# Differential attention: sums of softmax weights added on DVE before one product with ones, in a kernel of four layers

## The chip, the cores and the metric

The kernel runs on one core of a Trainium2 chip. The metric is the device time of one launch in microseconds, the median of several runs. Engines are named as in the profile: PE is TensorE (its weight loads are PEld), DVE is VectorE, ACT is ScalarE, POOL is GpSimd, SP is SyncE, which issues transfers.

## The reference

Four layers, each with a layer norm in front and a residual behind: a linear recurrence with gates (attn_a), a feed-forward layer with weights of three values (ffn), a differential softmax attention (attn_b), and the feed-forward layer again. Activations are 2 batches of 1024 rows by 512 features. The change touches attn_b alone:

```python
q = jnp.concatenate([q1, q2], axis=1)            # 32 query heads of 32
k2 = jnp.repeat(k, 2, axis=1)                    # 16 key heads, each used twice
v2 = jnp.repeat(v, 2, axis=1)
scores = jnp.einsum('bhqd,bhkd->bhqk', q, k2) * scale
scores = jnp.where(causal, scores, finfo.min)
p = jax.nn.softmax(scores, axis=-1)
y = jnp.einsum('bhqk,bhkd->bhqd', p, v2)
y1, y2 = (y[:, :H], y[:, H:])
lam = jax.nn.sigmoid(x @ Wlam)...
y = y1 - lam * y2
return y @ Wo
```

## The kernel before

The attention stage lies between about 734 and 1686 us of the span. It works through 32 *pairs* (`pairs`, L819), one for each batch b, group g of heads (four; two with q1, two with q2), p (which two of the group's key heads) and par (which of the group's two tiles of queries), four to a group. A sequence of 1024 is taken in key blocks kb of 128 and in two halves qb of queries. A pair has six *steps* of two key blocks each: two steps for the first half (qb = 0, kb 0 and 2) and four for the second (qb = 1, kb 0, 2, 4 and 6); the last two of a half lie at the diagonal.

In a step PE does, in this order, which is written out by hand for PE (`manual_schedule` of PE, L1298):

- the row phase (`row_phase`, L1002): scores into PSUM (L1024), then the row maxima subtracted by a product with ones (L1034). ACT takes the exponential into a tile of weights `pr` (L1056, four buffers); on blocks at the diagonal POOL cuts what is not causal (L1064); then POOL adds the weights of the second key block to those of the first (L1088);
- the banks of scores for the row maxima of the *following* pair (`maxima_bank`, L933, matmul L947), which DVE reduces (L958 with the causal mask on the diagonal, L963 without). `split_maxima` (L972; DVE L978 and L980, POOL L983 to L987) and `turn_maxima` (L990; PE transposes L994, DVE copies `mt` to SBUF in L996) hand them on;
- the weighing of the step before (`weigh`, L1091): products of the weights (first the second block's, then the added ones, except where kb is 0) with the values (tile `val`) into the first half of a PSUM bank, and a product of the added weights with ones (tile `summed`) into the second half, which gives the softmax's denominators. Both are L1109. After the last step of a query half ACT copies the bank (`ys`, L1128), and SP sends the denominators to `tot` (L1137) and the result to `share` (L1144);
- what is put beside a step by `at` (L1220 on): in two pairs of every group but the last, three projections each of queries or keys for the next group (`project`, L874, matmul pq L880) after steps 0, 2 and 4; transposes of the maxima; work of the second batch's input.

PSUM holds seven of these banks, handed out in rotation, so that a bank's next use waits for whoever reads it last. The orders of DVE, ACT, POOL and SP are decided by the framework's scheduler; only in the tail is DVE's written by hand too. At the end of a batch `divide` (L1149) turns the denominators into factors (DVE reciprocal L1156, multiply L1158, copy L1162, subtract L1163), `combine` (L1165) spreads them by a product `r` (L1170) over the shares (DVE L1173, POOL subtracts in L1174), and `project_part` (L1183, L1187) makes the output projection. `first_input` (L1199) prepares the input of the last layer in a room borrowed from the query buffers.

Outside this stage L224 and L514 to L519 belong to the first layers (quantizing weights, the recurrence).

Of the kernel before, what the change touches and what calls it, by code (L numbers as in the profile page):

```python
# [17 lines left out]
P = 128  # L18
D = 512
# [23 lines left out]
def kernel(  # L43
# [725 lines left out]
    with ExitStack() as s:  # L769
# [37 lines left out]
        for i in range(4):  # L807
# [10 lines left out]

        pairs = [  # L819
            (b, g, p, par)  # L820
            for b in range(NT // SEQ) for g in range(NG) for p in range(2) for par in range(2)
        ]
        groups, nmax, lams, totals, shares, factors = {}, {}, {}, {}, {}, {}

# [49 lines left out]
        def project(b, g, kind, e, w):  # L874


            n = f"{b}_{g}_{kind}"
            po = ring_bank(f"pq{n}_{e}")
            for k in range(NKC):
                nc.tensor.matmul(  # L880
                    po, w[:, k, ts(kind, P)], xts[b][:, k, ts(e, BLK)],
                    start=(k == 0), stop=(k == NKC - 1),
                )
            if e == 0:

                pool = (b_d, b_a, b_p)[kind]
                groups[b, g, kind] = pool.tile(
                    [P, 2, SEQ], F32, tag=f"group{kind}", name=f"gr{n}", bufs=2
                )
            made = groups[b, g, kind][:, :, ts(e, BLK)]  # L890
            if kind == 2:
                nc.scalar.copy(made[:, 0, :], po)
            else:
                nc.scalar.mul(made[:, 0, :], po, 1.0 / math.sqrt(HD))
            for i in range(2):
                nc.sync.dma_start(out=made[ts(i, 64), 1, :], in_=made[ts(1 - i, 64), 0, :])
# [7 lines left out]
        def name(pair):  # L904
# [19 lines left out]
        max_banks = [  # L924
# [6 lines left out]
        ]  # L931
# [70 lines left out]
        def row_phase(pair, following, step):  # L1002
# [47 lines left out]
            def weights(i, e):  # L1050
                if i not in room:
                    room[i] = b_a.tile(
                        [P, 2, BLK], F32, tag="pr", name=f"pr{name(pair)}_{made[i][0]}", bufs=4
                    )
                width = made[0][3] + made[1][3] if joined else made[i][3]
                nc.scalar.activation(room[i][:, e, :width], banks[i, e][:, :width], AF.Exp)  # L1056
# [27 lines left out]
                cut(1)  # L1084
            first, second = part(0), part(1)
            both = first[:, :, made[1][2] - made[0][2] :]
            for e in ((slice(0, 2),) if joined else range(2)):
                nc.gpsimd.tensor_add(both[:, e], both[:, e], second[:, e])  # L1088
            return [(pair, step, first, second)]

        def weigh(pair, step, first, second):  # L1091

# [5 lines left out]
                outs[pair] = edge_bank(f"y{name(pair)}_{qb}")  # L1098
            y, total = outs[pair][:, : BLK // 2], outs[pair][:, BLK // 2 :]
            last = kb == (qb + 1) * QB - 2  # L1100
            products = [(val[:, kb], first, lo0, y), (None, first, lo0, total)]
            products.insert(2 if kb == 0 else 0, (val[:, kb + 1], second, lo1, y))

            for n_product, (values_of, moving, lo, into) in enumerate(products):
                for half in range(2):
                    for e in range(2):
                        rows = ts(2 * half + e, HD)
                        head = summed if values_of is None else values_of[:, ts(4 * g + 2 * p + e, HD)]
                        nc.tensor.matmul(  # L1109
                            into[rows, lo // 2 :].rearrange("p (a r) -> p a r", r=64),  # L1110
                            head,
                            moving[:, e, :].rearrange("p (a h r) -> p a h r", h=2, r=64)[:, :, half, :],
                            start=(kb == 0 and n_product == 0),
                            stop=last and n_product > 0,
                            skip_group_check=True,
                        )
            if not last:
                return
            ys = b_c.tile([P, BLK], F32, tag="ys", name=f"ys{name(pair)}_{qb}", bufs=2)
            c = g % 2  # L1120
            if par == 0 and p == 0 and g % 2 == 0 and qb == 0:
                if g == 0:
# [20 lines left out]
            for half in range(2):  # L1143
# [2 lines left out]
                    in_=ys[ts(half, 64), : BLK // 2].rearrange("p (a r) -> p a r", r=64),  # L1146
                )

        def divide(b, e):  # L1149

            part = totals[b][:, ts(e, BLK)]

            pieces = 1 if b else NKC
            for i in range(pieces):
                piece = part[:, ts(i, BLK // pieces)]
                nc.vector.reciprocal(piece, piece)  # L1156
            second = part[rows_of[1]]
            nc.vector.tensor_mul(second, second, lams[b][rows_of[1], ts(e, BLK)])  # L1158
            factors[b, e] = b_c.tile([96 + NH, BLK], F32R, tag="factors", name=f"factors{b}_{e}")
            nc.gpsimd.memset(factors[b, e].bitcast(F32), 0.0)  # L1160
            hi, lo = (factors[b, e][64 * i : 64 * i + 32 + NH] for i in range(2))
            nc.vector.tensor_copy(hi, part)  # L1162
            nc.vector.tensor_sub(lo, part, hi.bitcast(F32))  # L1163

        def combine(b, c, e):  # L1165

            y1, y2 = (shares[b, half][:, c, ts(e, BLK)] for half in range(2))
            for half, y in enumerate((y1, y2)):
                r = ring_bank(f"r{b}_{c}_{e}_{half}")
                nc.tensor.matmul(  # L1170
                    r, head_of[:, half, c, :], factors[b, e], start=True, stop=True
                )
                nc.vector.tensor_mul(y, y, r)  # L1173
            nc.gpsimd.tensor_sub(y1, y1, y2)  # L1174

        def load_out(b):
            w_o = b_c.tile([P, NKC, D], F32, tag="w_vo", name=f"w_o{b}")
# [5 lines left out]
        def project_part(b, j, k, w_o, psum=ring_bank):  # L1183
            if k == 0:
                outputs[j] = psum(f"b_out{b}_{j}")
            po = outputs[j]
            nc.tensor.matmul(  # L1187
                po, shares[b, 0][:, k, ts(j, P)], w_o[:, k, :],
                start=(k == 0), stop=(k == NKC - 1),
            )  # L1190
            if k == NKC - 1:
                xi = xres[b * NQ + j]
                nc.vector.tensor_add(xi, xi, po)
# [26 lines left out]
        for n, pair in enumerate(pairs):  # L1220
# [4 lines left out]
                at(n + 1, 0, split_maxima, following, 1)  # L1225

            nb, ng = divmod(4 * b + g + 1, NG)
            if p == 0 and nb < NT // SEQ:
                def part(kind, e, nb=nb, ng=ng):
                    return lambda: project(nb, ng, kind, e, held["w", nb, ng])  # L1230
                if par == 0:
                    at(max(n - 1, 0), 0, lambda nb=nb, ng=ng: hold(("w", nb, ng), load_weights, nb, ng))

                for i in range(3):
                    at(n, 2 * i, part((2, 0, 1)[(3 * par + i) // 2], (par + i) % 2))
            if following:
                at(n, 4, turn_maxima, following, 0)
            if n:
                at(n, 0, turn_maxima, pair, 1)

            if g == 2 and p == 1 and b + 1 < NT // SEQ:
                if par == 0:
                    at(n, 0, normal_stats, b + 1)
                for t in range(4):
                    at(n, 2 * (t // 2), normalise, b + 1, 4 * par + t, ring_bank)
            if g == 3 and p == 1 and b + 1 < NT // SEQ:
                if par == 0:
                    at(n, 0, lambda b=b: hold(("v", b + 1), load_values, b + 1))
                else:

                    for j in range(NQ):
                        at(n + 1, 0, lambda b=b, j=j: values(b + 1, j, held["v", b + 1]))
                    at(n + 1, 0, lambda b=b: hold(("o", b), load_out, b))
                    at(n + 1, 1, divide, b, 0)
                    at(n + 1, 1, lambda b=b: lambdas(b + 1))
                    for c in range(NKC):
                        at(n + 1, 2 + c // 2, combine, b, c, 0)

                    at(n + 1, 3, divide, b, 1)
                    for c in range(NKC):  # L1260
                        at(n + 1, 4 + c // 2, combine, b, c, 1)

                    for j in range(NQ):
                        m, t = (n + 1, 5) if j < 2 else (n + 2, (j - 2) // 3)
# [132 lines left out]
```

## Time and profile before

| | us |
|---|---|
| median of 3 runs | 2048.32 |
| lowest and highest | 2045.67, 2051.11 |
| profiled execution | 2050.75 |
| its span | 2049.0 |
| PE busy in it | 2022.5 |
| POOL busy | 784.6 |
| DVE busy | 1101.0 |
| mean granted clock | 0.996 |

The span runs from the first to the last instruction of the profiled execution; 1.75 us of its time lie around it. A line of a group gives line, engine, operation, output and inputs with their sizes, how many, then busy time and mean duration, then the idle time of the engine ahead of them with who ended it. A line of the timeline gives start, duration, engine, line, operation, sizes and in brackets the idle time before it and who ended it; xN are N instructions that follow one another. Windows give for each stretch the length, the busy time of PE, PEld, DVE, ACT and POOL with numbers of instructions, then the granted clock, the share of the DMA engines and GB/s.

### The profile page before, as it was taken

The page shows a single profiled execution, that of the slowest core. Times are in us where ns is not written, and L with a number is a line of the kernel's source. Part 1 is how long each engine was busy: PE and PEld are TensorE (multiplying, and loading weights), DVE is VectorE, ACT ScalarE, POOL GpSimd, SP SyncE. Part 2 cuts the span into 40 slices and gives each one's busy share as a digit, 9 for nine tenths or more (in the row PEclk, how much of TensorE's full clock was granted, in tenths as well). Part 3 has the DMA queues.
Part 4 walks back from the last instruction along what each step waited for, and adds up shares of the span by engine and source line. Part 5 has one row for each costly group of instructions (what it writes and reads, how often), then busy time and mean ns, then how long its engine had stood idle before and what let it go on. Part 6 is the DMA issues. An engine that isn't in the chain of part 4 may idle for free.

```text
span 2049.0 us, 34958 instructions
## 1 busy us (share of the span) xinstructions
PE 2022.5 (99%) x13824; PEld 1290.9 (63%) x13832; DVE 1101.0 (54%) x2375; ACT 818.2 (40%) x1453; POOL 784.6 (38%) x1131
## 2 busy tenths in 40 slices
PE   8999999999999999999999999999999999999998
PEld 4444444788888854555555545565556648888887
DVE  5876868444344434555565556455556554343422
ACT  4444343234333422444444423254444513343433
POOL 1412323122222222666666635365657732222222
PEclk9999999999999999999999999999999999999999
DMA  7121212500000111111111101202110032000000
GB/s 278 65 92 62 88 57 80 222 0 1 1 1 1 37 48 34 48 28 43 28 43 28 43 9 39 60 22 51 25 30 15 15 149 103 21 1 21 0 21 21
DMA packets 77651, 99.14 MB, mean 48 GB/s; under 512 B 41520, under 2 KB 49840, under 8 KB 77488
## 3 DMA queue, kind: packets, MB, share of 16 engines
q1 hardware_dynamic: 77488, 96.92, 14.4%
q8 instruction: 108, 1.77, 0.4%
q14 instruction: 55, 0.45, 0.1%
HBM read 58.75 MB, written 16.78 MB: 37 GB/s over the span
## 4 chain that ended last, share of the span: by engine, by line
PE 92%; DVE 5%; POOL 1%; issue 1%; ACT 1%; DMA 0%; SPq 0%; DVEq 0%; ACTq 0%; POOLq 0%
PE g L664 11%; PE u L664 11%; PE f_out L685 11%; PE y L1109 11%; PE s L947 9%; PE pq L880 8%; PE t L1024 8%; PE pv L842 3%; PE pq L328 3%; PE a_out L546 2%; PE b_out L1187 2%; PE pv L328 2%; PE pa L328 2%; PE pg L328 2%; PE pk L328 2%; PE t L1034 1%
## 5 line engine op out<-in xcount | busy, mean ns | idle before, releaser
L1056 ACT ACTIVATE pr<-t 128x512 f32<-128x512 f32 (+1 forms) x640 | 306.6, 558 | 347.5 <-PE t L1034 294.2
L679 POOL TENSOR_TENSOR ssq<-ssq,sq 128x512 f32<-128x512 f32 x120 | 154.5, 1288 | 589.6 <-ACT sq L678 589.6
L1088 POOL TENSOR_TENSOR pr<-pr,pr 128x384 f32<-128x384 f32 (+1 forms) x256 | 287.1, 1132 | 121.5 <-ACT pr L1056 114.3
L963 DVE TENSOR_REDUCE nmax<-s 128x1 f32<-128x384 f32 (+1 forms) x320 | 183.2, 581 | 201.5 <-PE s L947 200.9
L958 DVE CUSTOM_DVE_ANT_0 s<-s,causal 128x512 f32<-128x512 f32 (+3 forms) x512 | 245.6, 506 | 54.0 <-PE s L947 49.6
L947 PE MATMUL s<-gr,gr 32*128 32x384 f32 (+3 forms) x1664 | 264.0, 480 | 1.9 <-DVE nmax L963 1.9
L670 DVE TENSOR_TENSOR h<-h,u 128x512 f32<-128x512 f32 x128 | 88.1, 688 | 317.5 <-PE u L664 305.4
L664 PE MATMUL g<-xs,w 128*128 128x512 f32 x1024 | 257.7, 394 | 0.0
L685 PE MATMUL f_out<-w,hs 128*128 128x512 f32 x1024 | 254.3, 390 | 0.3 <-DVE hs L673 0.3
L664 PE MATMUL u<-xs,w 128*128 128x512 f32 x1024 | 253.2, 389 | 0.0
L1024 PE MATMUL t<-gr,gr 32*128 32x512 f32 (+3 forms) x1536 | 224.3, 528 | 1.3 <-DVE nmax L963 1.3
L664 PEld LDWEIGHTS u<-xs,w 128*128 128x128 f32 x1024 | 192.2, 188 | 40.6
L685 PEld LDWEIGHTS f_out<-w,hs 128*128 128x128 f32 x1024 | 191.5, 188 | 40.7 <-DVE hs L673 1.1
L664 PEld LDWEIGHTS g<-xs,w 128*128 128x128 f32 x1024 | 190.0, 188 | 39.6 <-issue 1.0
L947 PEld LDWEIGHTS s<-gr,gr 32*128 32x128 f32 x1664 | 172.5, 186 | 45.5 <-issue 15.3
L1109 PE MATMUL y<-pr,val 128*32 128x256 f32 (+3 forms) x3072 | 188.1, 334 | 2.5 <-POOL pr L1088 1.9
L880 PE MATMUL pq<-b_xt,w_qk 128*128 128x512 f32 x384 | 176.0, 603 | 0.8 <-DVE nmax L958 0.8
L1064 POOL TENSOR_SCALAR_AFFINE_SELECT pr<-pr 128x256 f32<-128x256 f32 x256 | 101.9, 410 | 194.5 <-ACT pr L1056 190.9
L672 ACT CAST hs<-h 128x512 fp32r<-128x512 f32 x128 | 79.4, 620 | 234.7 <-DVE h L670 234.7
L669 ACT ACTIVATE h<-g 128x512 f32<-128x512 f32 x128 | 76.6, 599 | 230.5 <-PE g L664 230.4
L1109 PEld LDWEIGHTS y<-pr,val 128*32 128x32 f32 x3072 | 80.3, 109 | 89.4 <-issue 49.7
L673 DVE TENSOR_TENSOR hs<-h,hs 128x512 fp32r<-128x512 f32 x128 | 88.6, 692 | 87.2 <-ACT hs L672 87.2
(169 smaller groups left out, 2555.0 us busy)
## 6 DMA issues: line engine op xcount, KB each, us to landing
w<-w_kept SPq DMA_DIRECT2D x32, 768.0 KB
w_kept<-w SPq DMA_DIRECT2D x16, 768.0 KB
gr<-gr SPq DMA_DIRECT2D x96, 128.0 KB
w<-in_w_gu_dram SPq DMA_DIRECT2D x32, 256.0 KB
share<-ys SPq DMA_DIRECT2D x128, 64.0 KB
x<-in_x_dram SPq DMA_DIRECT2D x16, 256.0 KB
w<-in_w_pt_dram SPq DMA_DIRECT2D x16, 256.0 KB
w_qk<-in_wq_dram SPq DMA_DIRECT2D x8, 512.0 KB
```

The costliest lines, as they stand in the source:

```text
L328: nc.tensor.matmul(po, w[:, k, ts(c, P)], xt[:, k, :], start=(k == 0), stop=(k == NKC - 1))
L664: nc.tensor.matmul(po, ws[f][:, part, ts(k, P)], xs[:, e, k, :], start=(k == 0 and e == 0), stop=(k == NKC - 1 and e == 1),)
L679: nc.gpsimd.tensor_add(ssq, ssq, sq)
L685: nc.tensor.matmul(po[j], hp[:, e, ts(j, P)], ws[f][:, 2, :], start=(f == 0 and e == 0), stop=(f == NF - 1 and e == 1),)
L880: nc.tensor.matmul(po, w[:, k, ts(kind, P)], xts[b][:, k, ts(e, BLK)], start=(k == 0), stop=(k == NKC - 1),)
L947: nc.tensor.matmul(part, queries[:, ts(j, P)], keys[:, first * P : (first + nk) * P], start=True, stop=True,)
L958: nc.vector.tensor_tensor_reduce(part, part, causal[:, BLK - part.shape[-1] :], -1.0, 3.0e38, ALU.add, ALU.min, top,)
L963: nc.vector.tensor_reduce(top, part, AX.X, ALU.max, negate=True)
L1024: nc.tensor.matmul(banks[i, e][:, at_col : at_col + nq], keys[:, ts(kb, P)], queries[:, (qb + 1) * BLK - nq : (qb + 1) * BLK], start=True, ...
L1056: nc.scalar.activation(room[i][:, e, :width], banks[i, e][:, :width], AF.Exp)
L1088: nc.gpsimd.tensor_add(both[:, e], both[:, e], second[:, e])
L1109: nc.tensor.matmul(into[rows, lo // 2 :].rearrange("p (a r) -> p a r", r=64), head, moving[:, e, :].rearrange("p (a h r) -> p a h r", h=2, ...
```

## The change

For the second half of the queries the weights of steps 2 and 3 (kb = 0 and 2, full width) no longer have a product with ones each. `weigh` keeps the added weights of step 2 (`whole`), adds them to those of step 3 by a DVE add of 128x1024, and gives the sum one product with ones at the next step. The tiles `pr` therefore get six buffers. In the last pair DVE and not POOL adds the weights of the second block to the first (`adder`). The order of the pairs has par outside p; the projections stand in the second and third pair of a group; the query groups share three buffers and the key groups two. Two of the maxima steps have their banks in another order. The reciprocals are made in quarters (`invert`), placed step by step, and `combine` writes its difference into the other buffer (y2), which `project_out` reads.

```diff
-            for b in range(NT // SEQ) for g in range(NG) for p in range(2) for par in range(2)
+            for b in range(NT // SEQ) for g in range(NG) for par in range(2) for p in range(2)
...
-                pool = (b_d, b_a, b_p)[kind]
-                groups[b, g, kind] = pool.tile(
-                    [P, 2, SEQ], F32, tag=f"group{kind}", name=f"gr{n}", bufs=2
+                tag, bufs = ("keys", 2) if kind == 2 else ("queries", 3)
+                groups[b, g, kind] = b_p.tile(
+                    [P, 2, SEQ], F32, tag=tag, name=f"gr{n}", bufs=bufs
...
-            [(0, 0, "j4a"), (1, 0, "j01"), (0, 1, "j6a")],
-            [(1, 0, "j4a"), (0, 0, "j46"), (1, 1, "j5a")],
+            [(0, 0, "j4a"), (0, 1, "j6a"), (1, 0, "j01")],
+            [(1, 0, "j4a"), (1, 1, "j5a"), (0, 0, "j46")],
...
-                        [P, 2, BLK], F32, tag="pr", name=f"pr{name(pair)}_{made[i][0]}", bufs=4
+                        [P, 2, BLK], F32, tag="pr", name=f"pr{name(pair)}_{made[i][0]}", bufs=6
...
+            adder = nc.gpsimd if following else nc.vector
             for e in ((slice(0, 2),) if joined else range(2)):
-                nc.gpsimd.tensor_add(both[:, e], both[:, e], second[:, e])
+                adder.tensor_add(both[:, e], both[:, e], second[:, e])
...
+        whole = {}
...
-            products = [(val[:, kb], first, lo0, y), (None, first, lo0, total)]
-            products.insert(2 if kb == 0 else 0, (val[:, kb + 1], second, lo1, y))
+            sums = [(None, first, lo0, total)]
+            if qb and kb < QB:
+                sums = []
+            elif qb and kb == QB:
+                sums.insert(0, (None, whole.pop(pair), 0, total))
+            products = [(val[:, kb], first, lo0, y), *sums]
+            products.insert(len(products) if kb == 0 else 0, (val[:, kb + 1], second, lo1, y))
...
+            if qb and kb < QB:
+                if kb:
+                    nc.vector.tensor_add(first, first, whole[pair])
+                whole[pair] = first
...
+        def invert(b, e, i, pieces=NKC):
+            piece = totals[b][:, ts(e * pieces + i, BLK // pieces)]
+            nc.vector.reciprocal(piece, piece)
+
         def divide(b, e):
...
-            pieces = 1 if b else NKC
-            for i in range(pieces):
-                piece = part[:, ts(i, BLK // pieces)]
-                nc.vector.reciprocal(piece, piece)
...
-            nc.gpsimd.tensor_sub(y1, y1, y2)
+            nc.gpsimd.tensor_sub(y2, y1, y2)
...
-            room = b_d.tile([P, NKC, D], F32, tag="group0", name="xn_f1_0", bufs=2)
+            room = b_p.tile([P, NKC, D], F32, tag="queries", name="xn_f1_0", bufs=3)
...
-            if p == 0 and nb < NT // SEQ:
+            m = 2 * par + p
+            if m in (1, 2) and nb < NT // SEQ:
...
-                if par == 0:
-                    at(max(n - 1, 0), 0, lambda nb=nb, ng=ng: hold(("w", nb, ng), load_weights, nb, ng))
+                if m == 1:
+                    at(n - 1, 0, lambda nb=nb, ng=ng: hold(("w", nb, ng), load_weights, nb, ng))
                 for i in range(3):
-                    at(n, 2 * i, part((2, 0, 1)[(3 * par + i) // 2], (par + i) % 2))
+                    at(n, 2 * i, part((2, 0, 1)[(3 * (m - 1) + i) // 2], (m - 1 + i) % 2))
...
-                    at(n + 1, 1, divide, b, 0)
+                    for i in range(NKC):
+                        at(n, 3 + i // 2, invert, b, 0, i)
+                        at(n + 1, 1 + i // 2, invert, b, 1, i)
+                    at(n + 1, 1, divide, b, 0)
...
-        at(n, 3, divide, 1, 0)
+        for i in range(NKC):
+            at(n, 3 + i // 2, invert, 1, 0, i)
+        at(n, 5, divide, 1, 0)
...
             if c == 0:
                 combine(1, 2, 0)
                 combine(1, 3, 0)
+                invert(1, 1, 0, 1)
                 divide(1, 1)
```

More of the change, by code (lines that the diff above doesn't have):

```diff
@@ L1113, in weigh @@
                             start=(kb == 0 and n_product == 0),
-                            stop=last and n_product > 0,
+                            stop=last and n_product > 0 or values_of is None and last,
                             skip_group_check=True,
                         )
+            if qb and kb < QB:
+                if kb:
+                    nc.vector.tensor_add(first, first, whole[pair])
+                whole[pair] = first
             if not last:
@@ L1121, in weigh @@
             if par == 0 and p == 0 and g % 2 == 0 and qb == 0:
-                if g == 0:
+                if b not in totals:
                     totals[b] = b_c.tile([32 + NH, SEQ], F32, tag="tot", name=f"tot{b}")
@@ L1187, in project_part @@
             nc.tensor.matmul(
-                po, shares[b, 0][:, k, ts(j, P)], w_o[:, k, :],
+                po, shares[b, 1][:, k, ts(j, P)], w_o[:, k, :],
                 start=(k == 0), stop=(k == NKC - 1),
@@ L1239 @@
                 at(n, 0, turn_maxima, pair, 1)
-            if g == 2 and p == 1 and b + 1 < NT // SEQ:
-                if par == 0:
-                    at(n, 0, normal_stats, b + 1)
+            if g == 2 and m > 1 and b + 1 < NT // SEQ:
+                if m == 2:
+                    at(n, 5, normal_stats, b + 1)
                 for t in range(4):
-                    at(n, 2 * (t // 2), normalise, b + 1, 4 * par + t, ring_bank)
-            if g == 3 and p == 1 and b + 1 < NT // SEQ:
-                if par == 0:
+                    at(n + 1, 2 * (t // 2), normalise, b + 1, 4 * p + t, ring_bank)
+            if g == 3 and m > 1 and b + 1 < NT // SEQ:
+                if m == 2:
                     at(n, 0, lambda b=b: hold(("v", b + 1), load_values, b + 1))
@@ L1253 @@
                     at(n + 1, 0, lambda b=b: hold(("o", b), load_out, b))
+                    at(n + 1, 1, lambda b=b: lambdas(b + 1))
+                    for i in range(NKC):
+                        at(n, 3 + i // 2, invert, b, 0, i)
+                        at(n + 1, 1 + i // 2, invert, b, 1, i)
                     at(n + 1, 1, divide, b, 0)
-                    at(n + 1, 1, lambda b=b: lambdas(b + 1))
-                    for c in range(NKC):
-                        at(n + 1, 2 + c // 2, combine, b, c, 0)
                     at(n + 1, 3, divide, b, 1)
-                    for c in range(NKC):
-                        at(n + 1, 4 + c // 2, combine, b, c, 1)
+                    for e in range(2):
+                        for c in range(NKC):
+                            at(n + 1, 2 + 2 * e + c // 2, combine, b, c, e)
                     for j in range(NQ):
```

## The prediction

> **What bounds the kernel now.** The page comes first: busy time by engine, then the engine shares of the chain that ended last.
>
> ```profile
> PE 2022.5 (99%) x13824; PEld 1290.9 (63%) x13832; DVE 1101.0 (54%) x2375; ACT 818.2 (40%) x1453; POOL 784.6 (38%) x1131
> PE 92%; DVE 5%; POOL 1%; issue 1%; ACT 1%; DMA 0%; SPq 0%; DVEq 0%; ACTq 0%; POOLq 0%
> ```
>
> TensorE is the bound over the span, so a product less is time less, provided PE does not wait for what replaces it. The groups with shapes kept apart give the price of a product with ones, of POOL's add and of DVE's product of two SBUF tiles:
>
> ```profile
> L1109 PE MATMUL y<-pr,summed 128*32 128x256 f32 x1024 | 84.6, 383 | 0.0
> L1088 POOL TENSOR_TENSOR pr<-pr,pr 128x512 f32<-128x512 f32 x128 | 159.6, 1268 | 114.0 <-ACT pr L1056 113.9
> L514 DVE TENSOR_TENSOR mem<-mem,q 128x512 f32<-128x512 f32 x16 | 11.1, 692 | 0.6
> ```
>
> Matmuls overlap, so the 383 ns mean is no price. Start to start, eight records (one product at full width) take 0.43 us.
>
> The share of PE says nothing of slack inside a pair. For that I read the timeline of a pair that has no projection, 1608.13 to 1628.13; here is the stretch where the change puts its wait, PE's lines first, then DVE's, then POOL's:
>
> ```profile
> 1623.25 1.07 PE L1109 MATMUL y<-pr,val 128*32 128x256 f32 x16
> 1624.14 0.61 PE L1109 MATMUL y<-pr,summed 128*32 128x256 f32 x8
> 1624.68 0.40 PE L994 MATMUL mt<-ident,maxima 128*128 128x128 bf16 x4
> 1625.96 0.91 PE L947 MATMUL s<-gr,gr 32*128 32x256 f32 x7
> 1626.81 0.96 PE L1109 MATMUL y<-pr,val 128*32 128x192 f32 x16
> ...
> 1624.53 0.60 DVE L958 CUSTOM_DVE_ANT_0 s<-s,causal 128x384 f32<-128x384 f32 x1
> 1625.12 0.42 DVE L996 COPY mt_s<-mt 128x512 bf16<-128x512 bf16 x1
> ...
> 1621.11 2.50 POOL L1088 TENSOR_TENSOR pr<-pr,pr 128x512 f32<-128x512 f32 x2
> 1624.28 1.00 POOL L1088 TENSOR_TENSOR pr<-pr,pr 128x384 f32<-128x384 f32 x1
> 1625.60 0.99 POOL L1088 TENSOR_TENSOR pr<-pr,pr 128x384 f32<-128x384 f32 x1
> ```
>
> POOL's adds of step 3 end at 1623.61, and the products that read them start at 1623.68. POOL's adds of step 4 end at 1626.59, and their products start at 1626.81. DVE finishes the maxima of step 4 at 1625.13 and copies mt at once. PE is full here because all three engines are just in time; there is little room for a later DVE or POOL. Such a pair takes 20.0 us; one with three projections takes 29.7, of which 10.9 are projections (three of 3.6). The projections therefore cover about 1.2 us of waits per pair, which an uncovered pair already pays.
>
> **The change part by part.** *Removed:* in each of 32 pairs the ones products of steps 2 and 3, 0.43 us each. *Added on PE:* one product of the sum, 0.43, after step 4. Net 32 x 0.43 = 13.8 us, the most that this part can give.
>
> *Added on DVE:* one add of 128x1024 per pair, both inputs in SBUF. No row has the size. 128x512 takes 0.69 and the bf16 128x1536 product of L229 takes 1.76, so 1.22 by the line between them, an estimate (0.69 if the size cost nothing, 1.38 at twice the row). It stands in DVE's queue after the maxima of step 4 and before the mt copy; behind it wait the copy and the five maxima of step 5. PE's last maxima bank of step 5 takes the PSUM buffer that the copy empties, and the weighing of step 4 follows that bank.
>
> *14 pairs with projections (m of 1 or 2, all groups but the last).* A projection of 3.5 us lies on PE between the weighing of step 3 and step 5. It hides the add and the copy (1.64 together): -0.43 each, -6.0 us. Without this cover they would cost as the next ones do.
>
> *17 pairs without, the last pair apart.* I move the rows above. PE comes to the weighing of step 3 at 1622.82, and its second product at 1623.25 waits for POOL's add until 1623.61: 0.36 of the 0.86 saved is lost at once, and PE is 0.50 early. DVE's maxima of step 4 end at 1624.75, the add at 1625.97, the copy at 1626.39. PE wants the last bank at about 1625.85: 0.55 waited, so the weighing of step 4 starts at 1626.86 against 1626.81, and its extra product makes the pair about 0.45 longer. So much if DVE and POOL do not disturb each other. That they do is seen where POOL's L515 has a free DVE (first line) and where it lies beside a DVE operation of two SBUF inputs (last two):
>
> ```profile
> 84.24 1.26 POOL L515 TENSOR_TENSOR mem<-mem,v 128x512 f32<-128x512 f32 x1 [2.25 <-DVE mem L514]
> ...
> 67.38 2.71 POOL L515 TENSOR_TENSOR mem<-mem,v 128x512 f32<-128x512 f32 x1 [2.54 <-DVE mem L514]
> ...
> 67.22 1.75 DVE L224 SCALAR_TENSOR_TENSOR one<-scale,mag 128x1536 bf16<-128x1536 bf16 x1
> ```
>
> POOL loses 1.45 beside 1.75 of DVE, 0.83 of it. The new add lies wholly inside POOL's step-4 work, so POOL loses 1.22 x 0.83 = 1.0 and its last add ends at about 1627.6; the products that read it want it at 1627.3. That is 0.3 more, 0.8 us per pair, 17 x 0.8 = +13.6. If instead DVE loses (the 16x512 multiply of L1158 took 1.23 beside a POOL add and 0.68 alone, and the POOL cut behind it 0.86 in place of 0.41), the copy comes up to 1.0 later, one POOL add of 384: up to 1.8 per pair. Bounds: 17 x -0.43 = -7.3 if every wait falls into the 1.2 us that such a pair loses already, to 17 x 1.8 = +30.6. I take 0.8, because the row in which DVE starts first, as it does when its maxima end inside a POOL operation that has to start anew, is the nearest in operation and size.
>
> The Trainium skill, "SBUF — State Buffer", section "Who interferes with whom", gives the rule that speaks against this change: a DVE instruction with two SBUF inputs contends with a GpSimd instruction that reads SBUF, and by issue order one blocks fully, not partly. The L515 row agrees in kind, with 1.45 of 1.75 us. By the rule alone, with POOL's 384 add first, the copy would be 1.0 us later in every uncovered pair, and the sum would be near the upper bound.
>
> *Clock.* Granted clock was below full in two places only, each 6.83 us at half, about 3.4 us lost. One is this, by windows (PE busy first; the clock is the third number from the end):
>
> ```profile
> 1545.00:1550.00 5.00, 4.33 (x48) 2.32 (x47) 3.92 (x16) 2.44 (x5) 2.90 (x9) 0.81 0.00 0
> 1550.00:1555.00 5.00, 5.00 (x46) 3.07 (x46) 3.04 (x10) 0.87 (x2) 2.33 (x4) 0.51 0.12 27
> ```
>
> 0.67 us of idle PE in 5 us went before it, while 1185 to 1190 lost 1.15 and stayed at full clock. The new waits, 1.2 us per uncovered pair within 4 us, are of that size. Bounds: none (0) to all 17 (58 us). I take none, as most stretches of 82% busy or more in this stage show no drop, and let five (17 us) set the upper end.
>
> The Trainium skill, "TensorE: Matmul & The Clock Gate", Part 1, "What's actually happening", lets the clock fall after a whole idle window of some 3.4 us. The row disagrees: the clock fell with 0.67 us idle. By the page this term would be zero, by the row it can be several times 3.4.
>
> *Reciprocals in quarters, batch 0.* The first four stay where DVE had them (1188.68); those of the second half now lie beside 29 us of value and projection work. About 1 us that PE lost at 1254 to 1256 may go: -1 (0 to -1; the half clock at 1196.5 comes from the first four and stays).
>
> *Last pair.* POOL's adds go to DVE: 0.69 in place of 1.27, which brings PE 2.3 us forward by the weighing of step 2. But DVE then holds four reciprocals of 0.91 in the same queue as the adds. The totals land about 13.7 us into the pair (before, the one reciprocal of 3.34 waited 2.58 for them and nothing that PE needed stood behind it). From there 4 x 0.91, a multiply 0.68, an add of step 3 0.69, the sum 1.22 and two adds of 384 (0.55 each, between the 256 and 512 estimates) make 7.3, so 21.0; PE wants them at 17.2 and waits 3.8. Net about +1.7 (0 to +6, the upper with a half clock on top).
>
> *At nothing:* three query buffers and six weight buffers take no instruction; the other order of pairs moves the same loads on SP's queue, where a group's weights are still asked for one pair ahead of their use; the difference written into the other share buffer is the same POOL subtract, and lets batch 1's first share transfers on SP's queue start earlier, for which PE does not wait. If a weight load came late, PE would wait on w_qk, which it does not now.
>
> Sum: -6.0 + 13.6 - 1.0 + 1.7 = +8.3 us. The profiled execution took 2050.75 (span 2049.0), 2.4 above the median of 2048.32 and inside the runs (2045.67 to 2051.11), so I set the sum on the median: 2056.6, rounded 2057.
>
> **The rivals.**
> *Saving kept (faster).* The waits of an uncovered pair (0.56 in step 1 for a DVE copy, 0.40 in step 3 for an exponential) are not additional but absorb the new one. Then 31 x -0.43 = -13.3, -1 and a last pair of 0 to +1.7 give 2034 to 2036. For it: PE's chain is 92%. Against it: DVE's copy is on time by 0.3 us and the add takes 1.22. It decides if the DVE add takes under about 0.8 us or PE's last bank does not wait for the copy.
> *No contention.* POOL keeps its times: -6.0 + 17 x 0.45 - 1.0 + 1.7 = +2.4, 2051; no measurable change. For it: POOL's adds keep 1.27 beside the maxima of L958. Against it: those read PSUM and one SBUF tile, the add reads two.
> *Heavy waits.* DVE loses the boundary (+25: 2074) or five half clocks come on top of the sum (+25: 2074). For it: the L1158 rows and the drop after 0.67 us idle.
>
> **How the numbers follow.** Forecast 2057 with its own range 2053 to 2065: 0.37. Saving kept: 0.23. No contention: 0.22. Heavy: 0.18. About 0.3% (6 us) is what a measurement of this kernel can tell from no change: under 2042 is faster, over 2054.5 slower. Faster 0.23; same 0.22 with 0.03 of the forecast's lower edge, 0.25; slower 0.52. The range takes in the kept saving down to 2036 and heavy cases up to 2076.
>
> **What the new profile would show.** Right: L1109 ones records of full width down by 256, a DVE add of about 1.2 us in each pair, POOL L1088 of 384 longer than 1.00 in it, uncovered pairs of 20.8 us and covered ones of about 29.3, PE waiting on DVE's mt copy or POOL's pr in step 5, and in the last pair a wait of some 4 us. Wrong: uncovered pairs at 19.6 (the saving is kept), POOL rows unchanged (no contention), or many windows at a clock of 0.5 (heavy).

## The result, and the profile after

The changed kernel takes 2068.34 us (median of 5 runs, 2063.74 to 2070.15) against 2048.32 (2045.67 to 2051.11): 1.0094 times as long, 95% interval 1.0078 to 1.0111. The forecast was 2057, slower, with a range to 2076: the direction and the range held, the size did not; +20 us stand against +8.7. The profiled execution took 2066.13 (span 2064.4), which is 15.4 above that of before.

The page first, busy time by engine and the chain's shares:

```profile
PE 2033.0 (98%) x13576; PEld 1284.8 (62%) x13576; DVE 1149.4 (56%) x2420; ACT 817.8 (40%) x1453; POOL 805.5 (39%) x1121
PE 89%; DVE 6%; issue 2%; POOL 1%; DMA 1%; ACT 1%; SPq 0%; DVEq 0%; POOLq 0%; ACTq 0%
```

PE has fewer matmuls (13576 against 13824) and is busy 10 us longer, in part because it runs longer at half clock (below); its share of the chain is down by 3 points. In the groups by shape the intended part is all there:

```profile
L1117 PE MATMUL y<-pr,summed 128*32 128x256 f32 x768 | 58.9, 384 | 0.0
L1127 DVE TENSOR_TENSOR pr<-pr,pr 128x1024 f32<-128x1024 f32 x32 | 47.3, 1478 | 1.3 <-PE y L1117 1.3
L1064 POOL TENSOR_SCALAR_AFFINE_SELECT pr<-pr 128x256 f32<-128x256 f32 x256 | 118.2, 473 | 178.8 <-ACT pr L1056 171.5 <-PE t L1034 7.3
```

256 records with ones are gone; 32 adds came at 1478 ns each (1222 the shortest); POOL's cuts went from 410 to 473 ns.

Where the time went is best read by pairs. The table takes the start of each pair's first scores (L1024) in the trace of one execution of each kernel; the other columns are experiments told below ("both undone": both edits of the batch's end).

| us | before | changed | add left out | add if covered | both undone | final |
|---|---|---|---|---|---|---|
| pair without projections | 20.0 | 20.96 | 20.04 | 20.0 | 20.95 | 20.0 |
| pair with projections | 29.71 | 29.17 | 29.51 | 29.17 | 29.17 | 29.18 |
| pairs 15 to 18 | 170.9 | 176.4 | 176.9 | 176.2 | 173.1 | 171.1 |
| last pair | 21.65 | 24.44 | 22.56 | 23.85 | 24.32 | 19.65 |

So the plain pairs do what was forecast (+0.95 and -0.53 against +0.8 and -0.43). What was not forecast is the end of the first batch (+5.5), in part the last pair (+2.8), and the lower clock that is contained in both.

**A plain pair.** The pair from 1619.44 has the forecast's mechanism. Its timeline, PE, DVE and POOL, where the mt copy stands:

```profile
1636.79 0.86 PE L947 MATMUL s<-gr,gr 32*128 32x256 f32 x5
1637.81 0.91 PE L947 MATMUL s<-gr,gr 32*128 32x384 f32 x2
1638.64 0.96 PE L1117 MATMUL y<-pr,val 128*32 128x192 f32 x16
...
1635.89 1.53 DVE L1127 TENSOR_TENSOR pr<-pr,pr 128x1024 f32<-128x1024 f32 x1
1637.34 0.41 DVE L996 COPY mt_s<-mt 128x512 bf16<-128x512 bf16 x1
...
1635.34 1.00 POOL L1089 TENSOR_TENSOR pr<-pr,pr 128x384 f32<-128x384 f32 x1
1636.29 1.40 POOL L1064 TENSOR_SCALAR_AFFINE_SELECT pr<-pr 128x256 f32<-128x256 f32 x1
```

The copy follows the add at 1637.34 and ends at 1637.75; PE's last maxima bank starts at 1637.81, where in the kernel before it ran together with the five records before it (seven records from 1625.96). From the mt transposes to the weighing of step 4 PE needs 3.12 us in place of 2.13. The add begins beside a POOL add that runs to 1636.34 and takes 1.53 in place of 1.22; POOL's cut then lies beside the add and takes 1.40 in place of 0.40 (1625.23 in the kernel before). POOL's next add therefore ends at 1638.65, just as PE starts the products that read it (1638.64): behind the late copy, POOL has no time to spare either.

**The end of the first batch.** Pair 16 has a wait that the kernel before does not have:

```profile
1255.87 3.08 PE L947 MATMUL s<-gr,gr 32*128 32x512 f32 x4 [3.46 <-DVE share L1184]
...
1253.74 1.47 DVE L1173 CAST factors<-tot 48x512 fp32r<-48x512 f32 x1 [2.60 <-POOL factors L1171]
1255.14 0.67 DVE L1184 TENSOR_TENSOR share<-share,r 128x512 f32<-128x512 f32 x1
...
1250.75 2.50 POOL L1089 TENSOR_TENSOR pr<-pr,pr 128x512 f32<-128x512 f32 x2
1253.17 0.54 POOL L1171 MEMSET factors<- 112x512 f32 x1
```

The kernel before, PE's projection and DVE's cast:

```profile
1245.50 3.62 PE L880 MATMUL pq<-b_xt,w_qk 128*128 128x512 f32 x8
...
1255.45 1.86 DVE L1162 CAST factors<-tot 48x512 fp32r<-48x512 f32 x1
```

In the changed kernel DVE's cast of the second half's factors waits for POOL's memset, which stands behind two weight adds; two share multiplies and the maxima wait behind the cast, and PE waits for their banks. In the kernel before the cast stood behind all four multiplies of this step (1255.45), and a projection of 3.6 us in step 2 (1245.50) had held PE back while DVE and POOL came up. Right behind the changed kernel's wait the clock falls to half for 6.83 us (from 1256.1), about 3.4 of the 5.5 us by estimate; the kernel before has no fall here.

**The last pair.** DVE's queue and PE's two waits:

```profile
1653.65 0.94 DVE L1163 RECIPROCAL tot<-tot 48x128 f32<-48x128 f32 x1 [1.56 <-DMA tot<-ys]
1654.52 0.62 DVE L1089 TENSOR_TENSOR pr<-pr,pr 128x512 f32<-128x512 f32 x1
1655.06 2.55 DVE L1163 RECIPROCAL tot<-tot 48x128 f32<-48x128 f32 x3
...
1655.19 0.82 PE L1117 MATMUL y<-pr,val 128*32 128x256 f32 x6 [1.69 <-DVE pr L1089]
1660.41 1.23 PE L1117 MATMUL y<-pr,val 128*32 128x256 f32 x5 [1.70 <-DVE pr L1089]
```

The second add of step 3 stands behind a reciprocal that waits 1.56 us for its transfer, the adds of step 4 behind three more: 3.4 us of waits, as forecast (3.8). But then the clock fell to half. Windows (the clock is third from the end):

```profile
1655.00:1660.00 5.00, 3.52 (x26) 1.59 (x26) 4.93 (x7) 0.87 (x2) 1.52 (x3) 0.55 0.00 0
1660.00:1665.00 5.00, 4.59 (x49) 3.25 (x50) 2.38 (x5) 0.10 (x1) 0.53 (x1) 0.50 0.00 0
```

### The profile page after: what moved, and what is told of

It is laid out like the page before. It is cut to its first block, busy times and chain, and to the rows that moved or that the text cites. A ratio compares the mean times of both kernels' runs of the same rounds, so it can differ in the third digit from the quotient of the medians.

```text
span 2064.4 us, 34498 instructions
## 1 busy us (share of the span) xinstructions
PE 2033.0 (98%) x13576; PEld 1284.8 (62%) x13576; DVE 1149.4 (56%) x2420; ACT 817.8 (40%) x1453; POOL 805.5 (39%) x1121
## 4 chain that ended last, share of the span: by engine, by line
PE 89%; DVE 6%; issue 2%; POOL 1%; DMA 1%; ACT 1%; SPq 0%; DVEq 0%; POOLq 0%; ACTq 0%
PE g L664 11%; PE u L664 11%; PE f_out L685 11%; PE y L1117 9%; PE s L947 8%; PE pq L880 8%; PE t L1024 7%; PE pv L842 3%; PE pq L328 2%; PE a_out L546 2%; PE b_out L1198 2%; PE pa L328 2%; PE pv L328 2%; PE pg L328 2%; PE pk L328 2%
## 5 line engine op out<-in xcount | busy, mean ns | idle before, releaser
L1089 POOL TENSOR_TENSOR pr<-pr,pr 128x384 f32<-128x384 f32 (+1 forms) x248 | 291.9, 1187 | 116.2 <-ACT pr L1056 112.6
L947 PE MATMUL s<-gr,gr 32*128 32x384 f32 (+3 forms) x1664 | 273.3, 476 | 8.8 <-DVE share L1184 3.5
L963 DVE TENSOR_REDUCE nmax<-s 128x1 f32<-128x384 f32 (+1 forms) x320 | 177.3, 579 | 175.4 <-PE s L947 174.6
L1024 PE MATMUL t<-gr,gr 32*128 32x512 f32 (+3 forms) x1536 | 224.1, 526 | 0.0
L1064 POOL TENSOR_SCALAR_AFFINE_SELECT pr<-pr 128x256 f32<-128x256 f32 x256 | 118.2, 473 | 178.8 <-ACT pr L1056 171.5
```

The costliest lines, as they stand in the source:

```text
L947: nc.tensor.matmul(part, queries[:, ts(j, P)], keys[:, first * P : (first + nk) * P], start=True, stop=True,)
L963: nc.vector.tensor_reduce(top, part, AX.X, ALU.max, negate=True)
L1024: nc.tensor.matmul(banks[i, e][:, at_col : at_col + nq], keys[:, ts(kb, P)], queries[:, (qb + 1) * BLK - nq : (qb + 1) * BLK], start=True, ...
L1089: adder.tensor_add(both[:, e], both[:, e], second[:, e])
```

## The experiments

Three theories. *Queue:* what costs is the place of the add, and of the batch's and last pair's operations, in DVE's in-order queue. *Contention:* what costs is that a DVE add of two SBUF inputs and POOL exclude each other. *Clock:* most of the 20 us are half-clock stretches that short waits set off. Times below are medians, ratios to the kernel before on the same chip. Its medians on these occasions were 2049.4 to 2051.2, above the 2048.32 of the result, so a difference of two times from different occasions is uncertain by 1 to 3 us, and the ratios are the safer guide.

**Without the add.**

```diff
             sums = [(None, first, lo0, total)]
-            if qb and kb < QB:
-                sums = []
-            elif qb and kb == QB:
-                sums.insert(0, (None, whole.pop(pair), 0, total))
...
-            if qb and kb < QB:
-                if kb:
-                    nc.vector.tensor_add(first, first, whole[pair])
-                whole[pair] = first
```

> The changed kernel without the DVE add: every step has its product with ones again, all else as changed. Queue theory (the add stands in DVE's queue ahead of the mt copy and costs 0.95 us in each pair without projections, gains 0.53 in each with; the batch boundary and the last pair cost the rest): 18 x 0.95 - 14 x 0.53 = 9.7 us come back, 2068 - 10 = about 2058, uncovered pairs 20.0 and covered ones 29.7 again. Clock theory (most of the 20 us are half-clock windows that the add's waits set off): 2050 or below. If the order of pairs and the reciprocals were neutral: 2048.

Measured: 2060.77, ratio 1.0053 (1.0040 to 1.0065). Leaving the add out gives back 7.6 us (8.4 by the ratios), and the forecast's own terms for it, -6.0 and +13.6, had made +7.6. So the part that the change is about was sized about right; that the two numbers are equal is luck, as the table's pairs give 17 x 0.92 - 14 x 0.34 = 10.9. The other 10 us of the loss lie in the rest, which the forecast had at +0.7. That the add's waits set off most of the half clock (2050 or below) falls, and so does a neutral rest (2048). That the half clock makes up the rest does not fall: these runs have a mean granted clock of 0.992 against 0.997 of the kernel before beside them, and in the trace pairs 15 to 18, without any add, have 10.24 us at half clock from 1254.2.

**The add only where a projection covers it.**

```diff
+            covered = 2 * par + p in (1, 2) and 4 * b + g + 1 < 2 * NG
-            if qb and kb < QB:
+            if covered and qb and kb < QB:
...
-            elif qb and kb == QB:
+            elif covered and qb and kb == QB:
...
-            if qb and kb < QB:
+            if covered and qb and kb < QB:
```

> The DVE add and the single product only in the 14 pairs with projections, separate products in the others; all else as changed. Queue theory: covered pairs 29.17, uncovered 20.0, so 14 x 0.53 = 7.4 us below the run without the add: about 2051. If the saving in covered pairs is an accident of the trace: the same as the run without the add, 2058.

Measured: 2053.23, ratio 1.0015 (1.0006 to 1.0023): 7.5 us below the run without the add, 7.4 expected. The agreement is in part luck: against the run without the add a pair with projections gains 0.34 (29.51 to 29.17) and not 0.53, so 14 x 0.34 = 4.8 us; the remainder goes along with a higher mean clock (0.993 against 0.992). The saving is real wherever PE has a projection between the weighing of step 3 and step 5.

**One input in place of two, first try.**

```diff
-                    nc.vector.tensor_add(first, first, whole[pair])
+                    top = b_c.tile([P, 1], F32, tag="top", name=f"top{name(pair)}", bufs=2)
+                    nc.vector.tensor_reduce(top, first.rearrange("p e q -> p (e q)"), AX.X, ALU.max)
```

> In place of the add, at the same place in DVE's queue, DVE makes a maximum over the same 128x1024 weights of one tile (one SBUF input, a column out); the addition of the other tile is left out, so the denominators lack step 2. Queue theory: the operation takes about 1.2 and holds up the copy as before: uncovered pairs 20.7 to 20.96, about 2065 to 2068. Contention theory (the add and POOL's cut exclude each other: add 1.53 in place of 1.22, cut 1.40 in place of 0.41): the cut takes 0.41 again, POOL's adds end 1.0 earlier, uncovered pairs 20.3 or less, about 2057.

Measured: 2204.8, ratio 1.0755. The operation did not keep its place: as it writes no weights, it need not wait for PE to have read them, and the framework's scheduler put it ahead of DVE's maxima. There it waits for POOL:

```profile
996.07 1.22 DVE L1128 TENSOR_REDUCE top<-pr 128x1 f32<-128x1024 f32 x1 [2.09 <-POOL pr L1089]
...
998.14 0.91 PE L947 MATMUL s<-gr,gr 32*128 32x384 f32 x2 [2.19 <-DVE nmax L958]
```

The edit tells nothing of contention, but shows what a wrong place in this queue costs: 143 us more than the same work at the add's place (next run). About half of that, by estimate, is clock: with a wait of some 2.4 us in almost every pair (59.1 us in 25 waits up to 1650) the stage runs 167 us at half clock, against 31 in the next run.

**One input in place of two, at the add's place.**

```diff
-                    nc.vector.tensor_add(first, first, whole[pair])
+                    nc.vector.tensor_reduce(
+                        first[:, 0, :1], first.rearrange("p e q -> p (e q)"), AX.X, ALU.max
+                    )
```

> As the last run with a maximum in place of the add, but the result goes into a column of the same weights, so that the operation keeps the add's place in DVE's queue behind the maxima of step 4. The addition is left out. Queue theory: the maximum takes 1.2 in the add's place, the copy waits for it as before: uncovered pairs 20.6 to 20.9, about 2063 to 2067. Contention theory: POOL's cut takes 0.41 in place of 1.40 and the maximum 1.22 in place of 1.53; if POOL was what PE waited for, uncovered pairs 20.2 or less, about 2056.

Measured: 2061.63, ratio 1.0055 (1.0043 to 1.0067); plain pairs 20.63. DVE, then POOL:

```profile
1634.29 1.21 DVE L1127 TENSOR_REDUCE pr<-pr 128x1 f32<-128x1024 f32 x1
1635.42 0.41 DVE L996 COPY mt_s<-mt 128x512 bf16<-128x512 bf16 x1
...
1634.70 0.40 POOL L1064 TENSOR_SCALAR_AFFINE_SELECT pr<-pr 128x256 f32<-128x256 f32 x1
```

POOL's cut takes 0.40 beside it. The contention is real. Without it 0.33 of the 0.92 us go (20.96 less 20.63; 20.96 less 20.04), and the 0.59 that stay are the queue place and the operation's length. This does not yet price the contention alone, as the late copy still hides POOL's loss; the next run does. The Trainium skill, "SBUF — State Buffer", section "Who interferes with whom", says that a DVE instruction with at most one SBUF input, outside its 2-port modes, does not contend with GpSimd, and that one with two contends with a GpSimd instruction that reads SBUF; both rows agree (0.40 and 1.40 for the same cut).

**The copy ahead of the add.**

```diff
+                there = beside.get((n, step), [])
+                ahead = [x for x in there if step == 4 and x[0] in (split_maxima, turn_maxima)]
+                for f, args in ahead:
+                    f(*args)
                 for w in waiting:
                     weigh(*w)
```

> The changed kernel, but the split and the PE transposes of the first half of the maxima stand ahead of the weighing in step 4, so that DVE has the mt copy ahead of the add; the add stays as it is, two inputs and all. Queue theory: the wait of 0.99 us at PE's last maxima bank goes, uncovered pairs 20.0 to 20.4, 2068 - 17 x (0.6 to 1.0) = 2051 to 2058; some comes back if the add now delays the maxima of step 5. Contention theory: POOL's cut is still shut out by the add, uncovered pairs 20.7 or more, about 2064 to 2068.

Measured: 2062.53, ratio 1.0063 (1.0050 to 1.0077), plain pairs 20.70, between the two theories. The copy is no longer late, and POOL is. PE, then DVE, then POOL:

```profile
1634.91 0.42 PE L1117 MATMUL y<-pr,val 128*32 128x256 f32 x3 [0.34 <-POOL pr L1089]
...
1632.08 0.42 DVE L996 COPY mt_s<-mt 128x512 bf16<-128x512 bf16 x1
1632.41 1.22 DVE L1127 TENSOR_TENSOR pr<-pr,pr 128x1024 f32<-128x1024 f32 x1
...
1632.47 1.43 POOL L1064 TENSOR_SCALAR_AFFINE_SELECT pr<-pr 128x256 f32<-128x256 f32 x1
```

The cut loses 1.0 us to the add and PE waits for the add behind it. In the changed kernel the same loss of POOL lay hidden under the wait for the copy. Both limits are there; taking one away brings out the other: a plain pair loses 0.59 us with the contention away, 0.66 (20.70 less 20.04) with the copy ahead, 0.92 as changed.

**The last pair's order.**

```diff
-            at(n, 3 + i // 2, invert, 1, 0, i)
+            at(n, 4, invert, 1, 0, i)
...
-            adder = nc.gpsimd if following else nc.vector
+            adder = nc.gpsimd if following or step > 3 else nc.vector
...
+                if step == 3 and not n + 1 < len(pairs):
+                    ordered.enter_context(tc.manual_schedule(engines={mybir.EngineType.DVE}))
```

> The changed kernel; in the last pair alone, from step 3 on, DVE's order is that of the program (both adds of step 3, the sum, then the reciprocals that wait for the transfers), and POOL makes the adds of steps 4 and 5. Theory: the two waits of 1.7 us in the last pair come from adds standing behind the reciprocals, and the half clock that follows comes from them: last pair 24.4 to about 20.5 to 21, half-clock window gone, 2068 - 4 to -7 = about 2062. If PE waited for the exponentials anyway: 2067 or more.

Measured: 2066.11, ratio 1.0075 (1.0061 to 1.0088). The last pair takes 20.59 in place of 24.44, within the expectation, and less than before's 21.65. DVE, in the order now written out:

```profile
1660.19 1.23 DVE L1127 TENSOR_TENSOR pr<-pr,pr 128x1024 f32<-128x1024 f32 x1 [0.74 <-PE y L1117]
1661.34 3.37 DVE L1163 RECIPROCAL tot<-tot 48x128 f32<-48x128 f32 x4
```

In the kernel's time only 2.2 us show (3.9 by the ratios), which the intervals do not separate. In this profile the half clock behind the last pair's waits is down from 10.24 to 3.41 us, but more stretches elsewhere ran at half clock (24.42 for the first pair against 22.24, 29.53 for pair 15 against 27.20), in work that the edit leaves alone.

**Projections back in pair 16.**

```diff
+            lo = 0 if n // 4 == 4 else 1
-            if m in (1, 2) and nb < NT // SEQ:
+            if m in (lo, lo + 1) and nb < NT // SEQ:
...
-                if m == 1:
+                if m == lo:
```

> The changed kernel with the projections for the batch's second group in pairs 16 and 17, where the kernel before has them, in place of 17 and 18. Theory: pair 16 waits 3.5 us for DVE's share multiplies and then runs at half clock because no projection covers the division; pairs 15 to 18 give back 5 to 6 us: about 2062. Rival: the wait comes from the division's own order and stays, 2068.

Measured: 2068.72, ratio 1.0089 (1.0076 to 1.0102). No gain (pairs 15 to 18 take 179.1): the rival holds for this edit alone.

**The factors' tile zeroed once.**

```diff
-            factors[b, e] = b_c.tile([96 + NH, BLK], F32R, tag="factors", name=f"factors{b}_{e}")
-            nc.gpsimd.memset(factors[b, e].bitcast(F32), 0.0)
+            if e == 0:
+                factors[b, e] = b_c.tile([96 + NH, BLK], F32R, tag="factors", name=f"factors{b}")
+                nc.gpsimd.memset(factors[b, e].bitcast(F32), 0.0)
+            else:
+                factors[b, e] = factors[b, 0]
```

> The changed kernel, but the factors' tile is zeroed once in a batch and kept for the second half, so that DVE's cast does not wait for POOL's memset. Theory: the cast of pair 16 waited 2.60 us for that memset, which stood behind POOL's share subtract and weight adds, with the share multiplies and maxima queued behind it: the wait of 3.5 us goes, and the half clock: -3 to -7, about 2062 to 2065. Rival (cover is what is missing, not the memset): 2067 or more.

With the changed order of issue this edit also lets two of the four combinations of the first half read the second half's factors. Measured: 2066.55, ratio 1.0078 (1.0065 to 1.0092). Step 4 of pair 16 falls from 12.80 to 8.13, as the cast no longer waits, and step 5 rises from 12.71 to 15.63. The wait moved on; the time says no more than that.

**The division behind the multiplies.**

```diff
-                    at(n + 1, 3, divide, b, 1)
                     for e in range(2):
                         for c in range(NKC):
                             at(n + 1, 2 + 2 * e + c // 2, combine, b, c, e)
+                    at(n + 1, 3, divide, b, 1)
```

> The changed kernel with one line moved: at the end of the first batch the division of the second half is issued behind the share multiplies of the first, as in the kernel before. DVE's cast then stands behind all four multiplies and not between the second and the third. Theory (the cast, which waits for POOL's memset, holds the multiplies and maxima behind it): PE's wait of 3.5 us in step 4 of pair 16 goes, and its half clock with luck: step 4 from 12.8 to about 6 to 9, the kernel 2068 - 4 to -7 = about 2062. Rival (the missing cover): no change, 2067 or more.

Measured: 2068.90, ratio 1.0095 (1.0081 to 1.0110). A miss (pairs 15 to 18 take 177.7): the multiplies no longer stand behind the cast, but nothing lies on PE between them and the next use of the factors:

```profile
1254.67 2.05 PE L1181 MATMUL r<-factors,head_of 112*128 112x512 f32 x4 [3.00 <-DVE factors L1174]
```

**Order and cover together.** Both edits above.

> The changed kernel with both edits of the batch boundary undone together: projections in pairs 16 and 17, and the second division behind the share multiplies. Each alone moved the wait instead of ending it (order alone: PE waits 3.0 us for the factors; cover alone: the cast still holds DVE). Theory: together pairs 15 to 18 take about 171 us as in the kernel before, not 176: 2068 - 5 = about 2063, step 4 of pair 16 near 9.3. Rival (what holds PE there is the DVE add of step 3, 1.7 us or more beside POOL's share subtract): step 4 or 5 of pair 16 stays 2 us or more above the kernel before, 2066 or more.

Measured: 2062.82, ratio 1.0060 (1.0047 to 1.0073), 5.5 us under the changed kernel (7.0 by the ratios), 5 expected. Pairs 15 to 18 take 173.1 (171 expected), so 3.3 of it is seen there: the trace has no half clock at 1256 any more, and the wait for the factors is down to 1.05:

```profile
1259.65 1.17 PE L1181 MATMUL r<-factors,head_of 112*128 112x512 f32 x4 [1.05 <-DVE factors L1174]
```

The batch boundary needed both: projections beside the division, which give DVE and POOL time for it, and the division behind the multiplies. The change had moved the two at once, the first by its new places for projections, the second by the order of two lines of the plan.

**The pieces put together.** First the covered add, the last pair's order and the division behind:

> What the runs point to, together: the DVE add only in the 14 pairs with projections, DVE's order of the last pair as in the run on it, the division behind the share multiplies. From the run with covered sums (2053.2): last pair -3.5, pair 16 -3.5 to -7: about 2044, faster than both kernels. If the pieces hide one another: 2048 to 2052.

Measured: 2049.50, ratio 0.9998 (0.9989 to 1.0007): no better than before; the division, uncovered, still held PE for 2.9 us. Then with the projections in pairs 16 and 17 as well, and no add in pairs 16 and 18:

> The combined kernel (add only where a projection covers it, last pair's order, division behind) with the projections in pairs 16 and 17 as well, and no add in pair 16. Theory: pairs 15 to 18 lose their waits for the factors: the combined kernel's 2049.5 less 3 to 5: about 2045.5. Rival (the half clock at the boundary comes either way): 2049.

Measured: 2044.55 (2042.28 to 2046.14), ratio 0.9974 (0.9964 to 0.9985): faster than both kernels, 5 us below the one before on the same chip and 24 below the changed one.

## Why the prediction was right and wrong

- *The add in DVE's queue: about right.* Net of both kinds of pair +7.6 forecast; leaving it out gives 7.6 back (8.4 by the ratios), and the pairs alone make it 10.9: +0.92 each without projections against 0.8 forecast, -0.34 each with them against -0.43. The duration of 1.22 was exact where nothing disturbs it (shortest 1222 ns); over all 32 adds the median is 1479.
- *Who waits, and for what: half right.* The wait at the last maxima bank was forecast at 0.55 and a wait for POOL at 0.3 behind it. It was one wait of 1.0 for the copy, since DVE too lost 0.3 to POOL; POOL's 1.0 was lost but hidden. The sum, 0.8 against 0.92, came out near because the two errors offset each other, which is luck.
- *A step that failed: "Reciprocals in quarters, batch 0 ... -1".* I looked at the reciprocals alone and took the value and projection work beside them as cover. Behind them stand the cast, its wait for POOL's memset, and four multiplies, and I did not follow their order in DVE's queue; nor did I see that the new pair order takes the projections of steps 2 and 4 away from pair 16, where they gave DVE and POOL time for the division and its multiplies. Pairs 15 to 18 measured +5.5 in place of -1, about 3.4 of it half clock behind the new wait; undoing both parts takes 3.3 off these pairs and 5.5 off the kernel.
- *The last pair: right in its mechanism, short in its size.* Waits of 3.8 were forecast, 3.4 measured; +1.7 net became +2.8 in the pair, as the clock fell behind them. The order that avoids the waits takes the pair to 20.59, 1.1 under before.
- *The other step that failed, and the larger one: "Clock ... I take none".* The profile of before has 13.7 us at half clock in this stage, that of the changed kernel 23.9 (6.83 at 1194.7, 6.83 at 1256.1, 10.24 at 1655.5), so some 5 us in this one execution, contained in the pair times above. Over all runs it is more. The five runs of the changed kernel have a mean granted clock of 0.990 to 0.994, 0.9922 on average; 53 runs of the kernel before, beside the experiments, have 0.995 to 0.999, 0.9968 on average, and each 0.001 less goes with 1.7 us more there. The difference of 0.0046 is then worth 8 us, or 9.5 if it counted over the whole span: an estimate, and going along together is not yet cause. It would leave 10 to 12 of the 20 us for all else, where the sum without a clock term had 8.3.
- *Where the clock fell.* My worry was the 1 us waits of the plain pairs, and none of them set it off in the changed kernel's profile. The new stretches came behind the waits that I had not seen (pair 16) or had given a half clock only in a bound (last pair). The Trainium skill, "TensorE: Matmul & The Clock Gate", Part 1, "What's actually happening", asks for a whole idle window of about 3.4 us: the wait of 3.46 agrees, the fall at 1655.5 does not, where the wait ahead of it was 1.69.
- *What stays open.* The profiles differ by 15.4 us, the medians by 20.0: the profiled execution of before was 2.4 above its median, that of the changed kernel 2.2 below. The changed profile lost 2.4 more in the first 60 us, where both kernels do the same work: behind the same wait of PE of 2.06 us its clock fell (at 37.6) and that of before did not. So the same wait sets it off in one execution and not in another. No run here controls the clock, and leaving the add out or mending the last pair did not raise its mean (0.992 in both), so how much of the 20 us is due to the change's waits and how much to chance is left open.

## What to carry to other kernels

Work taken off the bound engine pays only where that engine has other work to lie over the substitute: the same add gained 0.34 us under a projection and lost 0.92 without one, so place it by the cover, not everywhere. When a step is moved, follow the whole in-order queue behind it, with each operation's foreign wait (a memset on another engine, a transfer), and ask which covering work was moved away with it. When one limit is taken away, expect the next at once, as with the copy and POOL's cut here.

## What the runs showed of the hardware

A DVE add of two SBUF inputs that begins beside POOL work costs both: the add went from 1.22 to 1.53 and the POOL cut from 0.41 to 1.40, while a DVE maximum of the same length with one SBUF input left the cut at 0.40. The clock fell to half after a wait of PE of 1.69 us (at 1655.5, last pair of the changed kernel) and stayed there for 10.24 us. After a wait of 2.06 us in the first layers it fell in the profile of the changed kernel (for 3.41 us from 37.6) and not in that of the kernel before. Waits of 1.0 us in the changed kernel's plain pairs never set it off in its profile; with waits of some 2.4 us in almost every pair (the misplaced maximum) 30 stretches at half clock came in the stage.
